# Attention slots of a pre-norm decoder layer: five slots for two chunks of four heads in place of three slots for each

## The chip, the cores and the metric

The kernel is one launch on one core of a Trainium2 chip, written in Bass with a tile framework. The metric is the device time of a launch in microseconds, the median of several runs; before the change it is 689.47 us (three runs, 688.49 to 689.93).

Engine names: PE is TensorE (its weight loads are listed apart as PEld), DVE is VectorE, ACT is ScalarE, POOL is GpSimd, SP is SyncE, whose queue issues most of the DMAs. A PSUM bank holds 512 float32 values in each of the 128 partitions here, and the kernel uses eight of them.

## The reference, cut to what matters

One decoder layer for a batch of 2, 512 tokens, width 1024: grouped causal attention with rotary positions (32 query heads, 8 key heads of 32 columns), a product of the quantised normalised tokens with a quantised context of 1024 x 1024, and a linear layer with eight low-rank experts.

```python
    qkv = x @ w_qkv.T + b_qkv
    q, k, v = jnp.split(qkv, [q_dim, q_dim + kv_dim], axis=-1)
    ...
    q = apply_rope(q, 0)
    k = apply_rope(k, 0)
    scores = jnp.einsum('bhqd,bhkd->bhqk', q, k) / math.sqrt(HEAD_DIM)
    scores = jnp.where(causal[None, None, :, :], scores, jnp.float32(-1e+20))
    attn = jax.nn.softmax(scores, axis=-1)
    out = jnp.einsum('bhqk,bhkd->bhqd', attn, v)
    return out @ w_o.T + b_o
...
x = x + _L0_attn_ref(_layernorm(x, axis=-1), ...)
x = x + _L0_xattn_ref(_layernorm(x, axis=-1), ctx_4096, ...)
x = x + _L0_ffn_ref(_layernorm(x, axis=-1), ...)
```

## The kernel before

**Stages.** The beginning (to about 47 us) loads and normalises the tokens of the first batch, turns them so that the contracted dimension lies on the partitions, and makes the first projections. Then the attention runs over 16 chunks `g`: chunk `g` is four query heads (of key heads that lie in the same four row groups) of batch `g // 8`. Behind it the tail makes the output product of the second batch, the products with the context and the feed-forward.

**A chunk.** `scores` makes, for each of the four query tiles `t` of 128 queries, the scores against the `(t + 1) * 128` keys that the causal mask leaves, for four heads side by side in four row groups of PE. DVE reads them from PSUM, adds the mask and keeps each row's least negated score (line 1018); ACT makes their exp for the row sums (line 1028). `split` turns minimum and log of the sum into three bf16 terms, and `turn_terms` transposes these (`tm`, line 1062). `weights` makes the scores again, transposed (keys on the partitions, line 1080), adds the terms with a small bf16 product (line 1088), and one exp on ACT then gives normalised weights `pt` for the whole slot (line 1097). POOL blanks the upper half of each diagonal block (line 1100). `attend` multiplies `pt` with the values for four heads in four column groups (`pv`, line 1122) and `evacuate` copies the result to `oT`.

**Slots.** One PSUM tile of four banks (`ps_sc`, one buffer), one bank for each head, serves scores and weights in turn. A chunk takes three slots of each kind. `QUERIES` says which query tiles a score slot holds: the tile of 512 keys, the tile of 384, and the tiles of 256 and 128 together. `KEYS` does so for the weights: key block 0 with 512 queries, block 1 with 384, blocks 2 and 3 with 256 + 128. So one slot in three is full. Three more banks (`ps_mm`) take projections and other products, one takes `pv`.

**The order** on PE, DVE, ACT and POOL is written out by the loop at the end: for each slot, `scores(g, j)`; in slot 1 the values of chunk `g - 2`; other PE work by `fill(rate * SLOT_S[j])`; the `weights` of four slots before; in slot 0 the `tm` of the chunk before; `fill(rate * SLOT_T[j])`; after the chunk its `split`. `fill` adds to a credit and calls `step` while it is positive; each `step` issues a matmul from a queue of generators and takes its cost from the credit. `hold(us)` issues further steps while the planner's clock of PE (class `Clocks`, which adds up estimated durations as instructions are issued) stands more than `HOLD` = 0.3 us ahead of the time that the next instruction's input will be ready. `need(key)` steps until a named piece of work is done. `dispatch` issues DVE and ACT pieces of side work ("lanes": additions of projections, the rotation, sums of weights and tokens, norms, quantising) once their inputs are ready by that clock.

**What fills the slots.** In the first half, the projections of the remaining query columns, keys and values by a scheme of seven products in place of eight: ("first", 2), then ("second", column), then ("third", 0 to 2) for the second batch, whose end issues the eight loads of `wo` on SP's queue; a product of a quarter has four matmuls of 128 x 512. In the second half, the output product of the first batch ("W"), column sums of the quantised context ("cs", which writes `corr`), turned tokens ("A", "X") and the context product ("C"). `FILL_1` and `FILL_2` give the us of such work that the two halves place by rate. At most `QBUFS` = 12 query tiles are held; a chunk gives its own back with its last `weights`.

The other names of the prediction: `pts` holds the weights of a slot, `ptp` their buffers, `q_live` counts query tiles, `cos_sb` and `sin_sb` are the rotation's factors, `beside` is a product of the tail that may fill the last slots.

Of the kernel before, what the change touches and what calls it, by code (L numbers as in the profile page):

```python
# [35 lines left out]
IN_ORDER = {  # L36
    getattr(mybir.EngineType, n) for n in ('PE', 'DVE', 'Activation', 'Pool')
}
NS = 3
QUERIES = ((3,), (2,), (1, 0))  # L40
KEYS = ((0,), (1,), (2, 3))

SLOT_S = (2.7, 0.0, 2.9)
SLOT_T = (1.4, 2.2, 1.8)
FILL_1 = 108
FILL_2 = 80.0


# [162 lines left out]
def kernel(  # L213
# [70 lines left out]
    def constant(shape, name, dtype=F32):  # L284
        return const.tile(shape, dtype, tag=name, name=name)
# [240 lines left out]
    def hold(us):  # L526

        while clocks.now("PE") + HOLD < us:
            if not (any_may() and step()) and next(last_resort[0], None) is None:
                break  # L530
# [289 lines left out]
    nc.sync.dma_start(bqk_sb, bqk)  # L820
    bv_sb = constant([P, 2], "bv_sb")
    nc.sync.dma_start(bv_sb, bv.rearrange("o (c p) -> p (o c)", p=P))
    cos_sb = constant([P, S], "cos_sb")
    nc.sync.dma_start(cos_sb, cos)
    sin_sb = constant([P, S], "sin_sb")
    nc.sync.dma_start(sin_sb, sin)
    load_q(left[0], 0)
    load_q(left[1], 1)
# [158 lines left out]
    def row(s):  # L987
        return slice(32 * s, 32 * s + 32)

    def scores(g, j):  # L990


        b, c = divmod(g, NC)
        if g not in stats:
            stats[g] = small.tile([P, NT, 4, 2], F32, tag="stats", name=f"stats{g}")
        sc = ps_sc.tile([P, 4, S], F32, tag="sc", name=f"sc{g}_{j}")
        parts = []
        at_col = 0
        for t in QUERIES[j]:
            klen = (t + 1) * P  # L1000
            part = slice(at_col, at_col + klen)
            at_col += klen
            parts.append((t, klen, part))
            for s in range(4):
                nc.tensor.matmul(  # L1005
                    sc[:, s, part],
                    qTs[b, c][row(s), t * P : (t + 1) * P],
                    kTs[b][row(s), c // 4, :klen],
                    start=True,
                    stop=True,  # L1010
                )
        last_sc[0] = sc
        for s in range(4):
            whole = msp.tile([P, S], F32, tag="ms", name=f"ms{g}_{j}_{s}")
            for t, klen, part in parts:
                ms = whole[:, part]
                least = stats[g][:, t, s, 0:1]
                nc.vector.tensor_tensor_reduce(  # L1018
                    out=ms,
                    in0=sc[:, s, part],  # L1020
                    in1=mask[:, S - klen :],
                    scale=-scale,
                    scalar=BIG,
                    op0=ALU.add,
                    op1=ALU.min,
                    accum_out=least,
                )
                nc.scalar.activation(  # L1028
                    ms,
                    ms,  # L1030
                    AF.Exp,
                    bias=least,
                    scale=-1.0,
                    accum_out=stats[g][:, t, s, 1:2],
                )
# [29 lines left out]
        mT[g] = rows.tile([P, S], BF16, tag="mT", name=f"mT{g}")  # L1065
        nc.scalar.copy(mT[g], ps.rearrange("p a b -> p (a b)"))

    def weights(g, j):


        b, c = divmod(g, NC)
        sc = ps_sc.tile([P, 4, S], F32, tag="sc", name=f"st{g}_{j}")
        parts = []
        n = 0
        for kb in KEYS[j]:
            parts.append((kb, slice(n, n + S - kb * P)))
            n += S - kb * P
        for kb, part in parts:
            for s in range(4):
                nc.tensor.matmul(  # L1080
                    sc[:, s, part],
                    kTs[b][row(s), c // 4, kb * P : (kb + 1) * P],
                    qTs[b, c][row(s), kb * P :],
                    start=True,
                    stop=False,
                )
            for s in range(4):
                nc.tensor.matmul(  # L1088
                    sc[:, s, part],
                    onesb[32 * s : 32 * s + 3, :],  # L1090
                    mT[g][32 * s : 32 * s + 3, kb * P :],
                    start=False,
                    stop=True,
                )
        last_sc[0] = sc
        pt = ptp.tile([P, 4, n], F32, tag=f"pt{j}", name=f"pt{g}_{j}")
        nc.scalar.activation(pt, sc[:, :, :n], AF.Exp, scale=scale)  # L1097
        for kb, part in parts:
            diagonal = pt[:, :, part.start : part.start + P]
            nc.gpsimd.affine_select(  # L1100
                out=diagonal,
                in_=diagonal,
                compare_op=ALU.is_ge,
                fill=0.0,
                base=0,
                pattern=[[0, 4], [1, P]],
                channel_multiplier=-1,
            )
        pts[g, j] = pt, parts
        weighted[0] += j == NS - 1  # L1110
        q_live[0] -= j == NS - 1

    def attend(g):

        b, c = divmod(g, NC)
        pv = ps_pv.tile([P, S], F32, tag="pv", name=f"pv{g}")
        for j in range(NS):
            pt, parts = pts.pop((g, j))
            for kb, part in parts:
                for s in range(4):  # L1120
                    h = 4 * (c // 4) + s
                    nc.tensor.matmul(  # L1122
                        pv[row(s), kb * P :],
                        vs[b][:, kb, h * HD : (h + 1) * HD],
                        pt[:, s, part],
                        start=(kb == 0),
                        stop=(kb == NT - 1),
                    )
        if b not in oT:
            oT[b] = act.tile([P, NC, S], F32, tag="act", name=f"oT{b}")  # L1130
        evacuate(oT[b][:, c, :], pv)
        attended[0] += 1
# [292 lines left out]
    def unit(key, deps, fn):  # L1425
        units.append((key, deps, fn))
# [261 lines left out]

    def chain_units(b, w_keys):

        unit(("cs", b), [("q2", b, i) for i in range(CTX // P)], lambda: g_columns(b))
        made["cs", b] = lambda: [corr[b]]
        for t in tiles:
            part = slice(t * P, (t + 1) * P)
# [134 lines left out]
        )  # L1829

    beside = second()
    slots = sum(SLOT_S) + sum(SLOT_T)
    rate = FILL_1 / (NC * slots + SLOT_S[0] + SLOT_T[0] + SLOT_S[1] + SLOT_T[1])
    for g in range(last + 1):
        for j in range(NS):
            at[0] = g + j / NS
            if g == last:
                last_resort[0] = beside
            if g == NC + 1 and j == 2:
                rate = FILL_2 / ((NC - 1) * slots + SLOT_S[2] + SLOT_T[2])  # L1840
            if g < last:
                if j == 0:
                    need(("q", g))
                    if g == NC // 2:
                        need(("k", 0, 1))
                    if g == NC:
                        need(("k", 1, 0))
                    if g == NC + NC // 2:
                        need(("k", 1, 1))
                scores(g, j)  # L1850


            if j == 1 and g > 1:
                if g - 2 == NC // 2:
                    for key in [("second", c) for c in COLUMNS] + [("values", 0)]:
                        need(key)
                if g - 2 == NC:
                    for key in [("third", i) for i in range(3)] + [("values", 1)]:
                        need(key)
                hold(when([pts[g - 2, n][0] for n in range(NS)]))  # L1860
                attend(g - 2)
            fill(rate * SLOT_S[j])
            now_kb = (g - 2, NS - 1) if j == 0 else (g - 1, j - 1)
            if now_kb[0] >= 0:
                hold(max(sc_free(), when([mT[now_kb[0]]])))
                weights(*now_kb)
            dispatch()
            if j == 0 and g:
                hold(when([terms[(g - 1) % 2]]))
                turn_terms(g - 1)  # L1870
            fill(rate * SLOT_T[j])
            hold(sc_free())
        if g < last:
            split(g)
        if g == 2:
            bias_lane(0, xt, lambda: bo_sb)

            def begin_ctx0():
                take_xn()
                take_xn()  # L1880
                raws = [xnp.tile([P, D], F32, tag="xn", name=f"ctx_raw{i}") for i in range(2)]
                load_ctx(0, raws, place_of(0), give_xn)

            lane((3, "ctx"), Hop("DVE", begin_ctx0, can=lambda: xn_free[0] == 2))
        if g == NC - 1:
            xs[0] = xt
            chain_units(0, all_of("W", 0))
            w_units(0)
            queue.append(("post", g_post()))
    weights(last - 1, NS - 1)  # L1890
    def run_some(n):
        for _ in zip(range(n), beside):
            dispatch()
# [196 lines left out]
```

## Time and profile before

| | us |
|---|---|
| median of three runs | 689.47 |
| profiled execution, its own time | 689.95 |
| its span, first to last instruction | 688.2 |
| PE busy | 658.9 |
| DVE busy | 505.7 |
| ACT busy | 316.1 |
| POOL busy | 94.1 |
| first score matmul | 46.6 |
| last value matmul starts | 419.4 |

The page shows one profiled execution. "Busy" is the time in which at least one instruction of an engine runs; matmuls overlap each other, so a matmul's own duration (some 0.59 us for a record of 128 x 512 float32) is longer than the step from one to the next (0.43 us). A float32 matmul shows as two records. In a group's line stand the source line, engine, operation, the tiles written and read, the shape, the count, then busy time and mean duration in ns, then the engine's idle time just before and what ended it. In a timeline line the start and the duration of a run of like instructions come first. The largest groups of the attention:

```profile
L1028 ACT ACTIVATE ms<-ms,stats 128x512 f32<-128x512 f32 (+3 forms) x256 | 140.3, 549 | 94.1 <-DVE stats L1018 92.5
L1018 DVE CUSTOM_DVE_ANT_0 ms<-sc,mask 128x512 f32<-128x512 f32 (+3 forms) x256 | 109.1, 486 | 47.0 <-PE sc L1005 42.9
L648 PE MATMUL pj<-xT,wq 128*128 128x512 f32 x192 | 91.2, 605 | 0.0
L1097 ACT ACTIVATE pt<-st 128x1536 f32<-128x1536 f32 (+1 forms) x48 | 76.3, 1589 | 18.2 <-PE st L1088 17.3
L1080 PE MATMUL st<-qT,kT 32*128 32x128 f32 (+3 forms) x512 | 50.4, 471 | 8.0 <-DVE stats L1018 7.8
L1005 PE MATMUL sc<-kT,qT 32*128 32x128 f32 (+3 forms) x512 | 48.0, 467 | 1.2 <-ACT pt L1097 0.2
L1122 PE MATMUL pv<-pt,v 128*32 128x128 f32 (+3 forms) x512 | 37.8, 436 | 0.0
```

### The profile page before, as it was taken

The numbers are of one execution on the slowest core, as the hardware profiler recorded it, in microseconds if no ns is written. First come the engines' busy times: TensorE is split into PE (matmuls) and PEld (weight loads), VectorE is DVE, ScalarE is ACT, GpSimd is POOL, SyncE is SP. The second block draws the span as 40 slices with busy tenths as digits, with TensorE's granted clock in tenths as the row PEclk, the third lists the DMA queues.
The fourth block names the chain that finished last, engine by engine and source line by source line (L and its number), as shares of the span: only waits on it lengthen the run. The fifth ranks groups of instructions, "written<-read, shape, count | busy, mean of one in ns | idle before, by whom it ended". The sixth has DMA issues, their size and how long they took to land.

```text
span 688.2 us, 9278 instructions
## 1 busy us (share of the span) xinstructions
PE 658.9 (96%) x3332; PEld 299.8 (44%) x3332; DVE 505.7 (73%) x1204; ACT 316.1 (46%) x728; POOL 94.1 (14%) x213
## 2 busy tenths in 40 slices
PE   5999999999999999999999899998999999999997
PEld 5753343434343334343443444444445444444443
DVE  5799999846689897757677664899869735633775
ACT  2246566667756777777676752357212000110100
POOL 2101123211221122212222131001001000000000
PEclk9999999999999999999999999999999999999999
DMA  9920000000021331000000025171000003000104
GB/s 296 327 51 0 1 1 1 31 1 31 1 80 45 104 142 62 1 1 1 1 1 1 2 95 208 65 305 62 30 1 0 0 31 122 1 0 0 62 0 183
DMA packets 25325, 40.45 MB, mean 59 GB/s; under 512 B 2112, under 2 KB 15424, under 8 KB 25280
## 3 DMA queue, kind: packets, MB, share of 16 engines
q1 hardware_dynamic: 24992, 38.82, 16.7%
q10 hardware_dynamic: 288, 1.05, 0.5%
q8 instruction: 26, 0.43, 0.2%
q14 instruction: 19, 0.16, 0.1%
HBM read 35.66 MB, written 4.19 MB: 58 GB/s over the span
## 4 chain that ended last, share of the span: by engine, by line
PE 63%; DVE 28%; ACT 4%; issue 2%; DMA 2%; POOL 0%; SPq 0%; DVEq 0%; ACTq 0%; POOLq 0%
PE wb L1573 14%; DVE ms L1018 10%; PE up L1656 7%; PE h L1620 7%; PE pj L648 6%; PE st L1080 4%; PE sc L1005 4%; PE pv L1122 4%; PE ct L1229 4%; PE wo L1229 3%; PE first_kv L648 2%; ACT pt L1097 2%; PE pj_v L648 2%; DVE qT L575 1%; DVE qT L639 1%
## 5 line engine op out<-in xcount | busy, mean ns | idle before, releaser
L1028 ACT ACTIVATE ms<-ms,stats 128x512 f32<-128x512 f32 (+3 forms) x256 | 140.3, 549 | 94.1 <-DVE stats L1018 92.5
L1018 DVE CUSTOM_DVE_ANT_0 ms<-sc,mask 128x512 f32<-128x512 f32 (+3 forms) x256 | 109.1, 486 | 47.0 <-PE sc L1005 42.9
L648 PE MATMUL pj<-xT,wq 128*128 128x512 f32 x192 | 91.2, 605 | 0.0
L1097 ACT ACTIVATE pt<-st 128x1536 f32<-128x1536 f32 (+1 forms) x48 | 76.3, 1589 | 18.2 <-PE st L1088 17.3
L1100 POOL TENSOR_SCALAR_AFFINE_SELECT pt<-pt 128x512 f32<-128x512 f32 x64 | 46.2, 734 | 249.1 <-ACT pt L1097 249.1
L1080 PE MATMUL st<-qT,kT 32*128 32x128 f32 (+3 forms) x512 | 50.4, 471 | 8.0 <-DVE stats L1018 7.8
L648 PEld LDWEIGHTS pj<-xT,wq 128*128 128x128 f32 x192 | 33.7, 190 | 39.5 <-issue 38.5
L1005 PE MATMUL sc<-kT,qT 32*128 32x128 f32 (+3 forms) x512 | 48.0, 467 | 1.2 <-ACT pt L1097 0.2
L1028 ACT ACTIVATION_READ_ACCUMULATOR ms<-ms,stats 128x1 f32 x256 | 47.8, 187 | 0.0
L1229 PE MATMUL wo<-wo,oT 128*128 128x512 f32 x96 | 47.1, 613 | 0.6 <-DVE x L1237 0.6
L1122 PE MATMUL pv<-pt,v 128*32 128x128 f32 (+3 forms) x512 | 37.8, 436 | 0.0
L1005 PEld LDWEIGHTS sc<-kT,qT 32*128 32x128 f32 x512 | 21.6, 183 | 36.5 <-ACT pt L1097 14.7
L1080 PEld LDWEIGHTS st<-qT,kT 32*128 32x128 f32 x512 | 20.1, 184 | 36.4 <-DVE stats L1018 26.8
L1229 PE MATMUL ct<-q,q1T 128*128 128x512 bf16 x128 | 30.7, 388 | 2.6 <-DVE x3T L373 2.4
L1573 PE MATMUL wb<-worg,x3T 128*128 128x512 f32 x64 | 28.3, 595 | 0.0
L1573 PE MATMUL wb<-worg,S 128*128 128x512 f32 x64 | 28.1, 592 | 0.0
L1573 PE MATMUL wb<-tb,S 128*128 128x512 f32 x64 | 27.9, 594 | 0.0
L1122 PEld LDWEIGHTS pv<-pt,v 128*32 128x32 f32 x512 | 15.0, 109 | 27.5 <-issue 23.8
L1229 PEld LDWEIGHTS wo<-wo,oT 128*128 128x128 f32 x96 | 16.4, 189 | 19.3 <-issue 17.7
L1632 ACT ACTIVATE hs<-h,coef 128x512 f32<-128x512 f32 x6 | 3.9, 686 | 43.1 <-PE h L1620 43.1
L639 DVE TENSOR_TENSOR qT<-pj,qT 128x512 f32<-128x512 f32 x28 | 18.8, 684 | 6.2 <-PE pj L648 6.2
L1594 DVE TENSOR_TENSOR x<-x,wb 128x512 f32<-128x512 f32 x24 | 15.5, 680 | 10.7 <-PE wb L1573 7.8
(243 smaller groups left out, 1063.2 us busy)
## 6 DMA issues: line engine op xcount, KB each, us to landing
wq<-in_wqT_dram SPq DMA_DIRECT2D x8, 512.0 KB, 8.3
ctx_raw<-in_ctx_dram SPq DMA_DIRECT2D x8, 512.0 KB, 3.3
wo<-in_woT_dram SPq DMA_DIRECT2D x8, 512.0 KB, 3.3
raw<-in_ctx_dram SPq DMA_DIRECT2D x8, 512.0 KB, 3.5
worg<-in_worgT_dram SPq DMA_DIRECT2D x8, 512.0 KB, 5.7
out_dram<-x SPq DMA_DIRECT2D x16, 256.0 KB, 2.1
x<-in_x_dram SPq DMA_DIRECT2D x7, 512.0 KB, 5.9
x_raw<-in_x_dram SPq DMA_DIRECT2D x4, 512.0 KB, 7.4
```

Source lines behind the costliest of these rows:

```text
L648: nc.tensor.matmul(ps[:, part], weight[:, k, :], xs_[:, k, part], start=(k == 0), stop=(k == n - 1),)
L1005: nc.tensor.matmul(sc[:, s, part], qTs[b, c][row(s), t * P : (t + 1) * P], kTs[b][row(s), c // 4, :klen], start=True, stop=True,)
L1018: nc.vector.tensor_tensor_reduce(out=ms, in0=sc[:, s, part], in1=mask[:, S - klen :], scale=-scale, scalar=BIG, op0=ALU.add, op1=ALU.min, ...
L1028: nc.scalar.activation(ms, ms, AF.Exp, bias=least, scale=-1.0, accum_out=stats[g][:, t, s, 1:2],)
L1080: nc.tensor.matmul(sc[:, s, part], kTs[b][row(s), c // 4, kb * P : (kb + 1) * P], qTs[b, c][row(s), kb * P :], start=True, stop=False,)
L1097: nc.scalar.activation(pt, sc[:, :, :n], AF.Exp, scale=scale)
L1100: nc.gpsimd.affine_select(out=diagonal, in_=diagonal, compare_op=ALU.is_ge, fill=0.0, base=0, pattern=[[0, 4], [1, P]], channel_multiplier=-1,
L1122: nc.tensor.matmul(pv[row(s), kb * P :], vs[b][:, kb, h * HD : (h + 1) * HD], pt[:, s, part], start=(kb == 0), stop=(kb == NT - 1),)
L1229: nc.tensor.matmul(ps, l[:, t * P : (t + 1) * P], r[:, cols], start=(k == 0), stop=(k == len(terms_) - 1))
L1573: nc.tensor.matmul(ps[i], l[:, k, i * P : (i + 1) * P], r(k), start=(k == 0), stop=(k == n - 1))
L1620: nc.tensor.matmul(ps[i], r(k)[:, i * P : (i + 1) * P], l[:, k, :], start=(k == 0), stop=(k == n - 1))
L1656: nc.tensor.matmul(ps[t], l[:, k, t * P : (t + 1) * P], r(k), start=(k == 0), stop=(k == n - 1))
```

## The change

Slots are numbered through, `i` from 0, five to a pair of chunks. `QUERIES` and `KEYS` now name (chunk of the pair, tile), so that a slot may hold tiles of both chunks: 512, 384 + 128, 256 + 256 (one of each chunk), 512, 384 + 128. Every slot is full. `scores(i)` and `weights(i)` take the slot's number; the weights run `LAG` = 4 slots behind the scores. `pts` is kept by chunk and key block; three buffers of `pt`, all 2048 wide now, serve the five slots (`j % 3`). A chunk's query tile counts as given back when all four of its key blocks are made.

The loop changes with it. The values of a chunk stand in slots 2 and 4 of a pair, now with a fill of 0.8 units between them and the weights; `tm` stands in slots 0 and 3, `split` after slots 2 and 4. New is a loop at positions 0 and 3: it steps until the projection of the chunk that begins two slots later is done (`made_by` names it, for chunks from the fifth on). The fills' sizes are set anew. `cos` and `sin` lie in one tile that shares its buffer with `corr`, and the unit "cs" that first writes `corr` therefore waits for all rotations.

```diff
-NS = 3
-QUERIES = ((3,), (2,), (1, 0))
-KEYS = ((0,), (1,), (2, 3))
+QUERIES = (((0, 3),), ((0, 2), (0, 0)), ((0, 1), (1, 1)), ((1, 3),), ((1, 2), (1, 0)))
+KEYS = (((0, 0),), ((0, 1), (0, 3)), ((0, 2), (1, 2)), ((1, 0),), ((1, 1), (1, 3)))
+NS = len(QUERIES)
+LAG = 4
-SLOT_S = (2.7, 0.0, 2.9)
-SLOT_T = (1.4, 2.2, 1.8)
-FILL_1 = 108
+SLOT_S = (2.7, 3.2, 0.8, 2.7, 0.8)
+SLOT_T = (1.8, 2.2, 2.2, 1.8, 2.2)
+FILL_1 = 116.0
 FILL_2 = 80.0
...
-    cos_sb = constant([P, S], "cos_sb")
+    trig = const.tile([P, 2, S], F32, tag="corr", name="trig")
+    cos_sb, sin_sb = trig[:, 0, :], trig[:, 1, :]
...
-    def scores(g, j):
+    def scores(i):
+        pair, j = divmod(i, NS)
...
-        for t in QUERIES[j]:
+        for n, t in QUERIES[j]:
+            g = 2 * pair + n
+            b, c = divmod(g, NC)
...
-    def weights(g, j):
+    def weights(i):
+        pair, j = divmod(i, NS)
...
-        for kb in KEYS[j]:
-            parts.append((kb, slice(n, n + S - kb * P)))
+        for m, kb in KEYS[j]:
+            parts.append((2 * pair + m, kb, slice(n, n + S - kb * P)))
             n += S - kb * P
...
-        pt = ptp.tile([P, 4, n], F32, tag=f"pt{j}", name=f"pt{g}_{j}")
+        pt = ptp.tile([P, 4, n], F32, tag=f"pt{j % 3}", name=f"pt{i}")
...
-        pts[g, j] = pt, parts
-        weighted[0] += j == NS - 1
-        q_live[0] -= j == NS - 1
+        for g, kb, part in parts:
+            pts[g, kb] = pt, part
+            if all((g, n) in pts for n in range(NT)):
+                weighted[0] += 1
+                q_live[0] -= 1
...
-        unit(("cs", b), [("q2", b, i) for i in range(CTX // P)], lambda: g_columns(b))
+        turned = [("q", n) for n in range(B * NC)] + [("k", n, h) for n in range(B) for h in range(2)]
+        unit(("cs", b), turned + [("q2", b, i) for i in range(CTX // P)], lambda: g_columns(b))
...
-    slots = sum(SLOT_S) + sum(SLOT_T)
-    rate = FILL_1 / (NC * slots + SLOT_S[0] + SLOT_T[0] + SLOT_S[1] + SLOT_T[1])
-    for g in range(last + 1):
-        for j in range(NS):
...
+    n_slots = last // 2 * NS
+    first_ends = NC // 2 * NS + LAG
+    extra = lambda a, b: sum(SLOT_S[i % NS] + SLOT_T[i % NS] for i in range(a, b))
+    rate = FILL_1 / extra(0, first_ends + 1)
...
+    def made_by(g):
+        b, c = divmod(g, NC)
+        if not b:
+            return ("second", c - NC // 2) if c >= NC // 2 else None
+        return ("third", 0 if c % 4 == 0 else 1 if c % 4 == 1 else 2)
...
+    for i in range(n_slots + LAG - 1):
+        pair, j = divmod(i, NS)
+        if i == n_slots:
+            last_resort[0] = beside
+        if i == first_ends + 1:
+            rate = FILL_2 / extra(i, n_slots + LAG - 1)
+        if i < n_slots:
+            if j in (0, 2):
+                begin_chunk(2 * pair + j // 2)
+            scores(i)
+        if j in (0, 3) and i + 2 < n_slots:
+            ahead = made_by(2 * pair + (1 if j == 0 else 2))
+            while ahead and ahead not in done:
+                step()
+        if j in (2, 4) and 2 * pair + j // 2 >= 3:
+            values_of(2 * pair + j // 2 - 3)
+        fill(rate * SLOT_S[j])
+        if i >= LAG:
+            of = {2 * ((i - LAG) // NS) + n for n, _ in KEYS[(i - LAG) % NS]}
+            hold(max([sc_free()] + [when([mT[g]]) for g in of]))
+            weights(i - LAG)
+        dispatch()
+        if j in (0, 3) and 0 < i <= n_slots:
+            g = 2 * pair - (j == 0)
+            hold(when([terms[g % 2]]))
+            turn_terms(g)
+        fill(rate * SLOT_T[j])
+        hold(sc_free())
+        if i < n_slots and j in (2, 4):
+            g = 2 * pair + j // 2 - 1
+            split(g)
```

`begin_chunk` and `values_of` are the old loop's `need` calls and its call of `attend`, given names. `attend` takes its four key blocks from `pts` one by one; its matmuls are the same.

## The prediction

> **What bounds the kernel now.** I read the page's busy times first, then the busy times in stretches of my own, then the timeline of TensorE (PE) through one chunk, then who waited for whom.
>
> ```profile
> PE 658.9 (96%) x3332; PEld 299.8 (44%) x3332; DVE 505.7 (73%) x1204; ACT 316.1 (46%) x728; POOL 94.1 (14%) x213
> ...
> 46.60:125.00 78.40, 75.89 (x425) 31.30 (x425) 74.90 (x206) 49.03 (x137) 14.13 (x30) 1.00 0.02 8
> 125.00:200.00 75.00, 74.35 (x472) 30.88 (x471) 49.41 (x155) 50.90 (x132) 16.34 (x41) 1.00 0.05 15
> 389.00:421.90 32.90, 29.80 (x242) 13.78 (x241) 17.89 (x48) 16.62 (x32) 9.07 (x18) 0.95 0.25 81
> 480.00:688.20 208.20, 204.19 (x562) 93.55 (x560) 134.27 (x206) 23.10 (x38) 2.20 (x4) 1.00 0.10 36
> ```
>
> The last four lines are stretches: length, then busy time of PE, weight loads, DVE, ACT and POOL, then the clock. The attention runs from the first score matmul at 46.6 us to the last value matmul at 421.7. PE is busy nearly throughout, in the attention and behind it, so every matmul costs its time wherever it stands. Moving a projection or an output product within the span gains nothing by itself. DVE is as full as PE only up to 125 us.
>
> "Busy" hides losses, so I made an account of steps. A float32 matmul of 512 columns has two records, and a record's step is 0.429 us (the feed-forward's 112 records take 48.07 us in the chain). Other widths are in proportion; bf16 takes half; four heads on four row or column groups run side by side. So charged, the matmuls from 46.6 to 421.9 make 316 us of 375. The other 59 us are what this change can reach; behind 421.9 only 4.4 us are lost. One chunk shows the first kind of loss:
>
> ```profile
> 159.86 0.93 PE L1005 MATMUL sc<-kT,qT 32*128 32x384 f32 x8
> 160.72 2.36 PE L1122 MATMUL pv<-pt,v 128*32 128x512 f32 x32
> 163.02 1.14 PE L1080 MATMUL st<-qT,kT 32*128 32x512 f32 x8
> 163.99 0.40 PE L1088 MATMUL st<-mT,onesb 3*128 3x512 bf16 x4
> 164.31 1.12 PE L648 MATMUL pj<-oT,t 128*128 128x512 f32 x2
> ...
> 171.74 2.84 PE L648 MATMUL pj<-xT,wq 128*128 128x512 f32 x6
> 174.52 1.14 PE L1005 MATMUL sc<-kT,qT 32*128 32x512 f32 x8
> 175.59 0.70 PE L648 MATMUL pj_k<-xT,wk 128*128 128x512 f32 x1
> ```
>
> Take starts, not durations (these overlap). Six projection records take 171.74 to 174.52, 2.78 us for 6 x 0.429 = 2.58: 0.20 lost. The scores take 1.07 for 0.86: 0.21 lost. So one visit to the 32-row mode costs PE **0.41 us** beyond its matmuls. In the slot where scores, values and weights follow each other (159.86 to 164.31) the losses are 0.22 + 0.15 + 0.22, and 0.20 in the projections beside it: **0.79** for one merged visit. A chunk has four single visits and one merged: 4 x 0.41 + 0.79 = 2.4, for 16 chunks 39 us.
>
> The second kind is waits. Idle time before PE's instructions, less the mode loss already counted, sums to 18.5 us in the attention: 9.0 for weights that wait for DVE's minima, 1.9 for scores that wait for the exp of the weights, 7.6 in seven single waits.
>
> ```profile
> PE st L1080 <- DVE stats L1018: 7.8, 11, 1.3
> PE ct L1229 <- DVE x3T L373: 2.4, 1, 2.4
> ...
> PE sc L1005 <- ACT pt L1097: 0.2, 1, 0.2
> ```
>
> (The view credits PE's own idle alone; the rest of each wait lies ahead of the first weight load or inside the 0.2 us of a mode change.) 39 + 18.5 leaves 1.5, which stands here:
>
> ```profile
> 170.72 0.93 PE L1080 MATMUL st<-qT,kT 32*128 32x384 f32 x8
> 394.89 1.49 PE L1080 MATMUL st<-qT,kT 32*128 32x384 f32 x8
> ```
>
> The same eight matmuls take 0.56 us more, just behind the 2.4 us wait of ct; the granted clock is 0.95 over that stretch, so some 3.3 us ran at half speed. The Trainium skill ("TensorE: Matmul & The Clock Gate", Part 1) puts the fall to half clock behind an idle window of about 3.4 us. Here 2.4 us of wait sufficed; by the rule such a wait costs only itself, by the row some 1.6 us more. My sum is the same by both, since I forecast no wait above 2 us.
>
> **The change part by part.**
>
> *Fewer, fuller slots.* Two chunks have 10 slots in place of 12, so 96 visits become 80. Columns, matmul instructions, DVE minima (256) and ACT exps of scores (256) stay. 16 visits x 0.41 = -6.6. But the merged visit is parted: before, the S-fill of that slot was 0.0; now 0.8 stands between values and weights. Scores with values cost 0.20 + 0.22 + 0.15 = 0.57 and the weights 0.41 more, 0.98 against 0.79: 16 x 0.19 = +3.0. Where a fill is skipped (below), the visit stays merged. I take **-3.6**, every visit parted; the other end is -6.6, none parted.
>
> *The exp of the weights.*
>
> ```profile
> L1097 ACT ACTIVATE pt<-st 128x1536 f32<-128x1536 f32 x32 | 46.2, 1444 | 10.3 <-PE st L1088 9.4
> L1028 ACT ACTIVATE ms<-ms,stats 128x384 f32<-128x384 f32 x64 | 38.6, 603 | 29.6 <-DVE stats L1018 29.6
> L1097 ACT ACTIVATE pt<-st 128x2048 f32<-128x2048 f32 x16 | 30.0, 1878 | 7.9 <-PE st L1088 7.9
> L1028 ACT ACTIVATE ms<-ms,stats 128x128 f32<-128x128 f32 x64 | 24.7, 386 | 0.0
> ```
>
> 32 x 1.444 + 16 x 1.878 = 76.2 becomes 40 x 1.878 = 75.1 on ACT, busy under half: 0 on the path. But scores and weights share the one buffer of four banks, so each turn is a chain: scores, minima, weights, exp, next scores. ACT starts 0.85 after the scores end (160.72 to 161.57 in the timeline); a 384 + 128 slot takes 4 x (0.60 + 0.39) = 3.96, the exp 1.88: next scores at 6.7 at the earliest. PE's cover with values in the slot: 2.30 + 0.8 x 1.137 + 0.4 + 1.29 + 2.2 x 1.137 = 7.4 (1.137 us of fill per unit: 116 over the 102 units of 25 slots; before, 108 / 94.3 = 1.145). Margin 0.7. Before, a 384 slot gave 0.85 + 4 x 0.60 + 1.88 = 5.1 against 2.30 + 1.29 + 2.2 x 1.145 + 0.2 = 6.3: margin 1.2. In this margin ACT also has context scalings of 1.24 us (8), row totals of 1.06 (4) and copies of 0.58. Behind the late exp stand the next scores, and every projection behind them on PE. Waits of this kind were 1.9 us; I take **+1.5**; ends 0 and +12 (0.5 for each of the 24 two-part slots).
>
> *Weights waiting for minima.* DVE needs 0.25 + 4 x 0.61 + 0.1 = 2.8 us for a 512 slot and 0.25 + 4 x (0.48 + 0.23) + 0.1 = 3.2 for a two-part slot. Cover in the value slot: before 2.3 for 2.3 (384 columns), nothing to spare, and 3.1 us of the 9.0 were lost in it; now 2.30 + 0.91 + 0.2 = 3.4 for 3.2. In the second half the rate was 80 / 81.7 = 0.98, so a 512 slot had 2.7 x 0.98 + 0.2 = 2.8 for 2.8, and 4.1 us were lost there; now it is 80 / 74.1 = 1.08, giving 3.1. I take **-4**, between -9 (all gone) and +4 (DVE's other work falls into a spare 0.2).
>
> *Projections two slots ahead.* Chunks from the fifth on have their projection finished at positions 0 and 3 of a pair. A quarter product is 8 x 0.429 = 3.44 us. Slot 18 wants 4 + 18 + 4 of them and 0.4 of transposes, 89.9; slot 20 four more, 103.6; slot 23 four more, 117.4. The rate has placed 74.1 x 1.137 = 84.3 before slot 18, 92.8 before 20 and 107.5 before 23: bursts of 6, 11 and 10 us on PE, right behind scores. They are the same matmuls sooner: 0. What they issue is also sooner: adds (0.68) and rotations (four of 0.7 to 0.8) on DVE, 49.4 of 75 us busy there; eight wo loads on SP's queue, whose products follow only after the seventh chunk's values; ctx loads stand behind them and feed column sums at 311 us. Then fills are skipped until the credit is repaid, and only the hold loops place work, which stop within 0.3 us of the planner's clock. Its error I put in the terms above.
>
> *Tiles and the rest.* cos and sin share a buffer with corr, whose first write must follow the last rotation, read last near 265 us and written near 314: 0; if late, another ready unit is taken. Queries are held four slots of 8.4 us in place of four of 7.5; the last projection pair needs four finished chunks, at slot 13, and is wanted by the rate at slot 14: 0, else a few tenths. Up to 125 us DVE has 3.5 of 78.4 us free, so a quicker PE there gains nothing: 3.5 x 78/375 = **+0.7**. The single waits (7.6) and the clock loss (1.6) I leave as they are, since another order brings others; -9 to +5.
>
> **Sum.** -3.6 + 1.5 - 4 + 0.7 = -5.4. The profiled execution took 689.95 us (span 688.2), so its like would be 684.5; it stands 0.5 above the median of 689.47, so I say **684.0**.
>
> **Rivals.**
>
> *ACT decides the turn (24%, slower).* The exps of two parts come last in every full slot, and the exp of the weights, then the scores, stand behind them. For it: margin down from 1.2 to 0.7, one score buffer. Against: ACT is busy 50.9 of 75 us, and the hold loops know its queue. At 0.5 us in 24 slots: +12 in place of +1.5, and half of the gain on minima gone: -3.6 + 12 - 2 + 0.7 = +7, so 696. It decides from about 0.3 us a slot (7 / 24).
>
> *The gain is swallowed (13%).* The parted visit gives back 3.0, the waits move but stay, and DVE, at 97% up to 125 us, takes the rest: 689.
>
> *More than forecast (8%).* Skipped fills keep values and weights merged, minima are never late, the ct wait with its half clock doesn't come back: -6.6 - 9 - 4 = -20, so 670.
>
> The forecast itself has 55%, with 679 to 688 as its own range. A difference within 0.2% (1.4 us) can't be told from none. Faster: 55 + 8 = 63%; same 13%; slower 24%. The range 678 to 695 leaves out most of the last rival and the far half of the first.
>
> **What would show it.** 40 exps of 2048 at 1.88 us; 0.41 per single visit and 0.57 for scores with values; pairs of chunks at 42 to 44 us; the last value matmul between 408 and 420 us. Waits for minima at about 5 us show the fills right; score waits on the exp above 8 us show the ACT rival. A wait over 2 us with the clock down behind it, or projections waiting for sums of DVE before 125 us, would make the forecast wrong.

## The result and the profile after

The changed kernel takes 683.64 us (median of four runs, 683.45 to 685.98) against 689.34 for the kernel before: ratio 0.9918, 95% interval 0.9903 to 0.9934. 684.0 was predicted. The profiled execution took 683.77 us with a span of 682.0, 6.2 less than the 688.2 before. The page's groups of the attention, with their new line numbers:

```profile
L1033 ACT ACTIVATE ms<-ms,stats 128x512 f32<-128x512 f32 (+3 forms) x256 | 140.2, 549 | 77.6 <-DVE stats L1023 77.6
L1103 ACT ACTIVATE pt<-st 128x2048 f32<-128x2048 f32 x40 | 74.8, 1871 | 33.6 <-PE st L1094 32.2
L1086 PE MATMUL st<-qT,kT 32*128 32x128 f32 (+3 forms) x512 | 49.4, 460 | 7.4 <-DVE stats L1023 7.4
L1010 PE MATMUL sc<-kT,qT 32*128 32x128 f32 (+3 forms) x512 | 45.8, 460 | 4.1 <-ACT pt L1103 2.1
```

40 exps of 2048 columns replace 48 of mixed size; ACT's exps of the scores and all matmul counts are the same. Who waited for whom on TensorE:

```profile
PE st L1086 <- DVE stats L1023: 7.4, 13, 1.0
...
PE sc L1010 <- ACT pt L1103: 2.1, 8, 0.6
PE pj_k L651 <- DVE qT L642: 2.0, 1, 2.0
PE sc L1010 <- DVE ratio L1053: 1.5, 1, 1.5
```

The waits of the weights for the minima (first line) hardly fell from 7.8. Two single waits of 2.0 and 1.5 us stand before 125 us, where the kernel before had one of 1.3. The stretches show where:

```profile
46.60:125.00 78.40, 72.04 (x417) 29.93 (x410) 71.69 (x204) 48.58 (x144) 13.38 (x29) 1.00 0.00 1
125.00:250.00 125.00, 122.59 (x780) 51.97 (x780) 96.23 (x282) 85.43 (x212) 26.86 (x64) 1.00 0.16 51
250.00:413.40 163.40, 155.13 (x1201) 68.51 (x1200) 109.87 (x335) 114.46 (x270) 40.69 (x90) 1.00 0.05 17
```

Up to 125 us PE is busy 72.0 of 78.4 us, where it was 75.9; DVE fell as well, from 74.9 to 71.7. Both engines idle more there. The last value matmuls start at 411.2 in place of 419.4.

The prediction's account of steps, made for both traces, closes the difference (the same step per column, so that what is left is loss on TensorE; the third column is the run without the ahead loop, below):

| loss on TensorE, us | before | after | no ahead loop |
|---|---|---|---|
| mode changes | 39.3 | 35.1 | 35.1 |
| waits before 125 us | 3.0 | 7.0 | 7.0 |
| weights for minima, later | 7.6 | 5.4 | 2.5 |
| scores for the exp, later | 1.8 | 3.6 | 2.0 |
| single waits, later | 6.1 | 5.0 | 5.2 |
| half clock behind the ct wait | 1.6 | 0 | 0 |
| beginning and tail | 9.5 | 6.7 | 8.2 |
| sum | 68.9 | 62.8 | 60.0 |

The sums differ by 6.1 and 8.9; the spans by 6.2 and 9.0 (688.2, 682.0, 679.2). "Later" means behind 125 us. What a mode change costs by itself is taken out of the waits. Some traces lack a few matmul records; gaps of that kind are left out of the waits here and below, so a line may be off by a few tenths.

### The profile page after: what moved, and what is told of

It is laid out like the page before. It is cut to its first block, busy times and chain, and to the rows that moved or that the text cites. A ratio compares the mean times of both kernels' runs of the same rounds, so it can differ in the third digit from the quotient of the medians.

```text
span 682.0 us, 9216 instructions
## 1 busy us (share of the span) xinstructions
PE 652.4 (96%) x3332; PEld 300.8 (44%) x3332; DVE 504.1 (74%) x1205; ACT 312.7 (46%) x719; POOL 93.7 (14%) x213
## 3 DMA queue, kind: packets, MB, share of 16 engines
q1 hardware_dynamic: 24992, 38.82, 17.1%
## 4 chain that ended last, share of the span: by engine, by line
PE 72%; DVE 14%; ACT 11%; issue 1%; POOL 1%; DMA 0%; SPq 0%; DVEq 0%; ACTq 0%
PE wb L1580 14%; PE pj L651 8%; PE up L1663 7%; PE h L1627 7%; PE wo L1580 7%; DVE ms L1023 6%; ACT ms L1033 6%; PE sc L1010 5%; PE wo L1236 5%; ACT pt L1103 4%; PE st L1086 4%; PE ct L1236 3%; PE first_kv L651 2%; PE pv L1129 2%; PE wo L1717 1%; PE pj_v L651 1%
## 5 line engine op out<-in xcount | busy, mean ns | idle before, releaser
L1103 ACT ACTIVATE pt<-st 128x2048 f32<-128x2048 f32 x40 | 74.8, 1871 | 33.6 <-PE st L1094 32.2
L1010 PE MATMUL sc<-kT,qT 32*128 32x128 f32 (+3 forms) x512 | 45.8, 460 | 4.1 <-ACT pt L1103 2.1
L1236 PE MATMUL ct<-q,q1T 128*128 128x512 bf16 x128 | 29.1, 379 | 0.2 <-DVE q1T L376 0.2
```

Of the source, the lines that this page charges most:

```text
L1010: nc.tensor.matmul(sc[:, s, part], qTs[b, c][row(s), t * P : (t + 1) * P], kTs[b][row(s), c // 4, :klen], start=True, stop=True,)
L1236: nc.tensor.matmul(ps, l[:, t * P : (t + 1) * P], r[:, cols], start=(k == 0), stop=(k == len(terms_) - 1))
```

## The experiments

The theory ("visits"): the gain is fewer stays of TensorE in the 32-row mode. A "stay" here is one unbroken run of scores or of weights, and a "return" a change back to matmuls over the full 128 x 128 array. Rivals: the order of the projections, or the fill between values and weights, or single waits that fell out well.

### What a visit costs where nothing else counts

```diff
             for i in range(2):
+                nc.tensor.matmul(ps[i][:, :P], ident[:32, :], ident[:32, :], start=True, stop=True)
                 for k in range(n):
```

The same line stands ahead of the `up` products.

> The changed kernel with one small matmul on 32 rows (128 columns, float32) ahead of each of the 42 product banks of the feed-forward, where TensorE alone sets the time and nothing waits for a turn; the real product overwrites it. Theory visits: 42 x (0.41 for the mode change + 0.215 for the columns) = 26 us more than the changed kernel, near 710. Rival (the 0.41 in the attention is operands and queues, not the mode): 42 x 0.215 = 9 us, near 693.

709.66 us. The span is 707.8, 25.8 above the changed kernel's: 0.61 for each of 42. The chain of this run, start, duration, work:

```profile
586.17 0.41 PE h L1626 x2
586.59 3.63 PE h L1628 x8
590.22 0.41 PE h L1626 x2
```

Eight records of 0.429 are 3.43 us; they take 3.63. The two small ones, 0.215 us of columns, take 0.41. So 0.20 + 0.20 goes to one change into the mode and back, with no operand to wait for. The rival with 9 us is out: the price used in the prediction needs no queue and no wait.

Nor is it the price of any short matmul put in between. In the kernel before, from 33 to 42 us, four records of transposes, 128 columns each over the full array, alternate with two projection records of 512 columns. One round takes 1.30 us (34.43 to 35.73 in the timeline), and its columns alone make 4 x 0.107 + 2 x 0.429 = 1.29.

### More visits inside the attention

```diff
             part = slice(at_col, at_col + klen)
+            if at_col and any_may():
+                step()
             at_col += klen
```

> The changed kernel with one piece of other work between the two parts of each of the 24 two-part score slots: no matmul more, 24 visits to the 32-row mode more. Theory visits: loss on mode changes 35 + 24 x 0.41 = 45 us and the time 683.6 + 9.8 = 693. Rival order: TensorE has room for it, as the attention's turn is set by the other engines, and the time moves by less than 3 us.

713.62 us, 20 more than the theory said. The mode part agrees: 23 more stays at 0.21 and 17 more returns to full width at 0.20 make 8.2 us, and the account shows 7.6. But waits in the attention grew from 21 to 33, and by the trace's clock records four stretches of 3.4 us ran at half speed, behind waits of 2 to 3 us. The longest waits of this run:

```profile
PE st L1088 <- DVE stats L1025: 9.9, 12, 3.1
...
PE ct L1238 <- DVE x L1244: 3.5, 3, 1.8
PE pj_k L651 <- DVE qT L642: 3.0, 1, 3.0
```

The inserted work also delays the second part's scores, hence DVE, ACT and the next turn. So the turn is not slack: what lengthens it is paid too. A dose in the attention does not measure a visit alone; the one in the tail does.

### The ahead loop, taken out and alone

```diff
-        if j in (0, 3) and i + 2 < n_slots:
-            ahead = made_by(2 * pair + (1 if j == 0 else 2))
-            while ahead and ahead not in done:
-                step()
```

> The changed kernel without the loop that finishes projections two slots ahead. Theory visits (the gain is fewer visits of TensorE to the 32-row mode): the loss on mode changes stays at 35 us, waits differ by single ones, time 683.6 within 2 us. Rival order (the gain comes from where the projections stand): the waits grow and the time goes back to 687 to 690.

682.02 us, ratio 0.9877 (0.9856 to 0.9899), the fastest of all kernels here: below the changed kernel's interval, though each was measured beside its own runs of the kernel before. Mode changes are the same 35.1, as the theory said, and the order rival is wrong in its sign: without the loop the kernel is faster. The table's third column shows why: waits for minima behind 125 us fall from 5.4 to 2.5 and waits for the exp from 3.6 to 2.0, while 1.9 us of scores waiting for rotations and 1.5 in the tail come back. The profiled executions differ by 2.8 us, the medians by 1.6. In the changed kernel's timeline:

```profile
236.00 1.15 PE L1010 MATMUL sc<-kT,qT 32*128 32x256 f32 x16
237.07 2.36 PE L1129 MATMUL pv<-pt,v 128*32 128x512 f32 x32
240.22 1.14 PE L1086 MATMUL st<-qT,kT 32*128 32x512 f32 x8 [0.78 <-DVE stats L1023]
```

Scores, values and weights follow each other with no projection between, and the weights wait 0.8 us. The 0.8 units of fill were not placed: by the kernel's code a burst spends the credit, and a slot that took 14 us with a burst stands just ahead (213.6 to 227.7). Values run straight into weights in 10 of the 16 value slots, in 6 without the loop. Where the fill is placed, in the run without the loop, the weights do not wait:

```profile
187.27 2.36 PE L1129 MATMUL pv<-pt,v 128*32 128x512 f32 x32
189.56 1.12 PE L651 MATMUL pj_k<-xT,wk 128*128 128x512 f32 x2
190.62 1.14 PE L1086 MATMUL st<-qT,kT 32*128 32x512 f32 x8
```

In the kernel before, the loop alone, two slots ahead:

```diff
+            if j == 1 and g + 1 < last:
+                ahead = made_by(g + 1)
+                while ahead and ahead not in done:
+                    step()
```

> The kernel before with only the loop that finishes a chunk's projection two slots ahead. Theory visits: loss on mode changes stays at 39 us, time 689.3 within 2 us. Rival order: time 684 to 686, a good part of the whole change's gain.

691.22 us, ratio 1.0003 (0.9984 to 1.0022). The order of instructions is the same as without it: at 12.6 us of fill per chunk (11.0 x 1.145) the projections are done in time anyway, and the loop finds nothing to do. At the changed kernel's 11.6 (10.2 x 1.137) it does. The run is thus a repeat of the kernel before, and shows no gain from this part.

### The fill between values and weights

```diff
-SLOT_S = (2.7, 3.2, 0.8, 2.7, 0.8)
-SLOT_T = (1.8, 2.2, 2.2, 1.8, 2.2)
+SLOT_S = (2.7, 3.2, 0.0, 2.7, 0.0)
+SLOT_T = (1.8, 2.2, 3.0, 1.8, 3.0)
```

> The changed kernel with the 0.8 units of fill between values and weights moved behind the weights, so that scores, values and weights follow each other in 16 slots as before. Theory visits: loss on mode changes falls by up to 16 x 0.19 = 3 us from 35, less what is merged already; waits of the weights for the minima rise by at most 16 x 0.3 (what the hold loop leaves) = 5 us; time 681 to 686. Rival minima (the fill between them is what the gain rests on): waits for minima double from 8 to 16 us and the time is 690 or more.

684.82 us, ratio 0.9918 (0.9903 to 0.9933), the same. Mode loss 34.4 (-0.7), waits for minima 9.4 (+1.1): values meet weights directly in 12 slots in place of 10, so this edit had little left to change. In the kernel before, the other way round:

```diff
-SLOT_S = (2.7, 0.0, 2.9)
+SLOT_S = (2.7, 0.8, 2.1)
```

> The kernel before with SLOT_S = (2.7, 0.8, 2.1): 0.8 units of fill between values and weights, as the changed kernel has, taken from the third slot. By the prediction's terms: mode changes +3.0 us (39 to 42) and waits for minima 9.0 down to about 6, so the time stays within 2 us of 690. Rival (parting the visit is what makes the changed kernel faster): waits fall by more than 5 us and the time by 3 us or more.

703.31 us: neither. Within the attention it went as the prediction's terms say, in smaller size: mode loss up by about 1.2, waits for minima from 9.0 to 7.0. What cost 14 us stands in the tail (TensorE's clock was also halved for 17.1 us there, from within this wait on):

```profile
PE ta L1332 <- DVE a_b L1278: 14.6, 1, 14.6
```

The attention ended at 411 us with 7.3 us less fill in it, so the first batch's output product, its quantised rows and their transposes came when TensorE had nothing else to do. So the constants' choice can cost more than all mode changes that five slots save.

### The second half's constant

Only `FILL_2`, 80 in both kernels, is changed.

> The kernel before with FILL_2 = 76 in place of 80: the same slots and visits, a little less of the second half's work placed inside the attention. Theory visits: loss on mode changes stays at 39 us, and the time moves only by single waits at the end of the attention and the beginning of the tail. Rival order (the changed kernel's gain is that such single waits fell out well): some value of this constant gives the kernel before 684 or less. Expected 686 to 696.

687.51 us, ratio 0.9953 (0.9936 to 0.997): faster than the kernel before by a little more than half of what the change brings. Mode loss 39.4; the ct wait is 1.4 us at its longest and no half clock follows.

> The kernel before with FILL_2 = 86. As with 76: mode changes 39 us; 686 to 694 by the theory of visits, 684 or less by the rival of the order.

697.65 us, ratio 1.0101 (1.0079 to 1.0124), worse than expected. Waits in the tail are 5.6 us, and two stretches of 6.8 us ran at half clock.

> The changed kernel with FILL_2 = 86 in place of 80. Theory visits: mode changes 35 us, waits of the first 250 us unchanged, the time 681 to 688, below the kernel before at the same constant by 3 us or more. Rival order: 688 or more, no better than the kernel before at the same constant.

687.26 us, ratio 0.9939 (0.9916 to 0.9963); its profiled span is 683.7, 1.7 above the changed kernel's, with a wait of 2.1 us in the tail. Mode loss 35.4. At this constant the change is worth 10.4 us (697.65 to 687.26), at 80 it is worth 5.7; the changed kernel with 76 was not run.

Mode loss is the same in all, 39 with six slots and 35 with five. Neither 76 nor 86 brought the kernel before to 684, so the order rival is not enough at the values tried, but it is not nothing either: the best profiled spans are 685.9 with six slots, 682.0 with five and 679.2 with five and no ahead loop.

### The hold loops and the first stretch

```diff
-HOLD = 0.3
+HOLD = 0.0
```

without the ahead loop:

> The kernel without the ahead loop, and with HOLD at 0.0 in place of 0.3, so that the hold loops place work until the planner's clock meets the input. Theory planner (the remaining waits for minima and for the exp, 7.4 us in the run without the ahead loop, are what the hold loops leave): they fall to 3 to 5 us and the time by 2 to 4 us against that run. Rival (the other engines are later than the planner believes, by more than 0.3 us at a few places): waits and time stay within 1.5 us.

692.95 us: worse than both theories. Waits for the exp fell from 2.0 to 1.5, but those for minima rose from 5.3 to 8.4, one of 3.3, and the work that the loops pulled forward was missing at the end, where ct waits for DVE (4.4 us) and values for POOL (2.0). Behind waits of 3.1 and 2.0 us, stretches of 3.4 and 6.8 us ran at half clock; the run without the edit has no such stretch in the attention. So the planner's 0.3 alone does not explain the waits.

The sums of tokens on POOL, all 16 (`nc.gpsimd` and the lane's engine for `nc.vector`), without the ahead loop:

> The kernel without the ahead loop, and with the 16 sums of tokens (about 0.65 us each, 10 us) made by POOL in place of DVE. Theory full DVE (the 7.0 us of TensorE waits before 125 us, 2.9 in the kernel before, come from a DVE that is full there): they fall to 3 us or less and the time to 678. Rival late sums: POOL makes them later than DVE did, projections wait for them, and the time is 683 or more.

685.83 us. TensorE's waits for DVE before 125 us fell from 7.0 to 1.9, but the first chunk's terms stood behind the sums on POOL:

```profile
PE tm L1070 <- POOL terms L1064: 6.3, 1, 6.3
```

And with half of them there:

```diff
+            engine = "Pool" if i in (1, 4) else "DVE"
...
-                lane((0, "S"), Hop("DVE", lambda k=k: fn(k), can=can, **last))
+                lane((0, "S"), Hop(engine, lambda k=k: fn(k), can=can, **last))
```

> The kernel without the ahead loop, with 8 of the 16 sums of tokens on POOL (1.4 us each there, 11 us, ending before the first chunk's terms need POOL). Theory full DVE: TensorE waits before 125 us fall from 7.0 to 3 us or less, and no wait for POOL takes their place: 4 us faster than the kernel without the ahead loop, near 678. Rival: waits for late sums or for POOL of 3 us or more, time 682 or above.

683.45 us, ratio 0.9901 (0.9871 to 0.9931): no gain. One wait of scores, 5.6 us, for minima that stood behind DVE's sums took the place of the others, and 6.8 us there ran at half clock. DVE's own sums in this run, POOL's beside them, and DVE's in the run without the edit, from three timelines:

```profile
56.17 4.64 DVE L543 TENSOR_TENSOR xT<-xT,xT 128x512 f32<-128x512 f32 x4
60.73 6.77 DVE L543 TENSOR_TENSOR oT<-xT,xT 128x512 f32<-128x512 f32 x4
```

```profile
57.01 6.61 POOL L793 TENSOR_TENSOR xT<-xT,xT 128x512 f32<-128x512 f32 x4 [22.11 <-DVE xT L543]
```

```profile
58.71 2.49 DVE L543 TENSOR_TENSOR oT<-xT,xT 128x512 f32<-128x512 f32 x4
```

A sum takes DVE 0.62 us alone and 1.7 while POOL makes sums. So the waits there do come through DVE's queue, as both runs move them, but POOL can't take the work over.

## Why the prediction was right

**The time and the direction** hold, and the main term is shown: the mode's price by a run that isolates it, its count by both traces. It explains 4.2 of the 6.2 us between the two spans. The other terms sum to -2.0 where -1.8 was forecast, but not one by one, and that part of the hit is luck (below). **Mode changes** were put at -3.6 and came to -4.2: stays fell from 96 to 80, returns to full width from 84 to 80, so 16 x 0.21 + 4 x 0.20 = 4.2, with the two halves of the 0.41. The bound of -6.6 was not reached, as the values were parted from their neighbours. But the 0.8 parted fewer than forecast: values ran straight into weights 15 times before and still 10 times after. More were parted in front, by work that the hold loop placed there: scores ran straight into values 13 times before and 6 after.

**The exp of the weights**: +1.5 forecast, +1.8 measured. The ACT rival did not come: margin was left, and score waits stayed at 3.6, far under its 8.

**Weights waiting for minima**: -4 forecast, -2.2 behind 125 us, and -0.7 in all. Here the step that failed is "Then fills are skipped until the credit is repaid, and only the hold loops place work ... Its error I put in the terms above": the bursts were priced at nothing, but the skipped fills are the very cover on which the -4 rested. Without the loop the waits fall by 5.1 behind 125 us and by 3.7 in all, near the forecast. The bursts cost 2.9 us on minima and 1.6 on the exp; 1.7 came back elsewhere (waits for rotations and one in the tail), which leaves the 2.8 that the spans of the profiled executions show. The run takes the bursts away with all that they move, so this sharing out is read from the two traces.

**Up to 125 us**: +0.7 forecast, +4.0 measured. The term priced only a gain that a full DVE ("3.5 of 78.4 us free") would take back, and no new waits. But DVE is less busy after the change than before, and TensorE waits more: 1.6 us more for scores whose queries had just been rotated, 1.5 for minima, 0.6 for an addition, 0.5 for a sum. The forecast's own sign against it, projections waiting for sums there, came with this last one, in a small size. The addition frees a projection's bank. It stands behind four minima of 0.61 in DVE's queue in both kernels. In the kernel before:

```profile
68.26 0.68 DVE L639 TENSOR_TENSOR qT<-pj,qT 128x512 f32<-128x512 f32 x1
69.00 0.38 PE L1062 MATMUL tm<-identb,terms 128*128 128x128 bf16 x4 [1.35 <-DVE qT L639]
```

After the change DVE makes it 1.4 us later, soon idles 2.9 us until the next scores, and ends the rotation (line 578) for the scores at 84.14 late; the view names `ratio`, the instruction just behind it:

```profile
69.62 0.69 DVE L642 TENSOR_TENSOR qT<-pj,qT 128x512 f32<-128x512 f32 x1
70.36 1.98 PE L651 MATMUL pj_k<-xT,wk 128*128 128x512 f32 x4 [1.97 <-DVE qT L642]
75.60 0.56 DVE L1023 CUSTOM_DVE_ANT_0 ms<-sc,mask 128x384 f32<-128x384 f32 x1 [2.89 <-PE sc L1010]
83.30 0.69 DVE L578 TENSOR_TENSOR qT<-qT,sh_q 128x512 f32<-128x512 f32 x1
84.14 1.14 PE L1010 MATMUL sc<-kT,qT 32*128 32x512 f32 x8 [1.51 <-DVE ratio L1053]
```

The two engines wait for each other in turn. Which part of the new order causes the +4.0 stays open: the two runs on POOL only show that the waits pass through DVE.

**Single waits and the clock**: left at 0 with ends of -9 and +5. The ct wait with its half clock did not come back, nor did a 2.0 us wait in the tail: -1.1 in the attention, -1.6 of half clock and -2.8 in the beginning and the tail, together -5.5. Minima and the first stretch, forecast at -3.3, came to +1.8, which is 5.1 worse. So the sum of these terms was met by pieces that the forecast had left at 0, which is luck. That 76 in place of 80 alone brings the kernel before more than half of the gain shows how loose this term is; the range had taken it in.

**Rivals**: "the gain is swallowed" is out by the interval; the 97% that it gives DVE up to 125 us is PE's share, DVE's was 74.9 of 78.4 us, 96%. "More than forecast" named the right pieces (the ct wait and its half clock went), but minima stayed late.

**Signs**: the exps, the price of a visit and the last value matmul came as forecast. Waits for minima were 8.3 us in place of about 5. Pairs of chunks, from first scores to first scores, took 38.1 to 49.8 us, and only three of seven lay within 42 to 44; the longest, from 213.6 us, holds a slot of 14 us with a burst.

## What to carry to other kernels

Count stays in a tile mode, not matmuls: where TensorE is full, each stay cost 0.41 us here with its return, and packing slots pays by that number, less where two stays shared a return (0.26 a stay in this change), in hand before anything is built. A rule that finishes work early by stepping ahead of a paced fill also spends the cover of the next waits; look at who stood behind that fill. And when the end of one stage feeds a chain in the next, change its pacing constant alone first: here that moved the same kernel by 10 us.

## What the runs showed of the hardware

A wait of TensorE of about 2 us may or may not be followed by half clock: the 2.4 us wait before ct was, and so was one of 1.8 us before weights in the kernel before with SLOT_S = (2.7, 0.8, 2.1); in the changed kernel neither the 2.0 us wait at 68 us nor any other was. In the clock records every stretch at half speed within a kernel lasts 3.4 us or a multiple (17.1 from within the 14.6 us wait on). The Trainium skill ("TensorE: Matmul & The Clock Gate", "What's actually happening") puts the fall behind an idle window of about 3.4 us; the length of the stretches agrees with its window, the waits of 2.4 and 1.8 us that sufficed do not.

DVE and POOL alternate at two-input sums. A sum takes 0.62 us on DVE alone; in the run with half of the sums on POOL each engine ends one every 1.67 us, in turn (DVE at 59.14, 60.81 and 62.49 us, POOL at 58.59, 60.26 and 61.94). The Trainium skill ("SBUF — State Buffer", "SBUF: two separate sides") describes a port pair that a DVE instruction with two SBUF inputs, or a GpSimd instruction, holds for its whole length while the other waits; the alternation agrees.
